# A four-layer graph network on one core: the blocks between layers 1 and 2 as a pipeline of sections in program order, with the normalized input stored and reloaded and the bias added by TensorE

## The chip, the core and the metric

The kernel runs on one core of one Trainium2 chip. TensorE (PE) multiplies matrices and writes to PSUM; VectorE (DVE), ScalarE (ACT) and GpSimd (POOL) work element by element on 128 partitions; SyncE (SP) issues DMAs, as ScalarE and GpSimd can. The engines run side by side, each through its own list of instructions in a fixed order, and wait for one another by semaphores. The metric is the device time of one execution in microseconds (us), as the median of several runs.

## What is computed

12,500 nodes with 128 features and 200,000 edges go through four layers. Each normalizes its input, cuts it at zero, passes messages along the edges and adds the result to its input:

```python
h = jnp.maximum(_layernorm(x, axis=-1), 0.0)
x = x + _L1_gnn_ref(h, edge_attr_3, edge_weight1, L1_gnn_Wq, ..., L1_gnn_Wo, L1_gnn_bo, L1_gnn_ln_g, L1_gnn_ln_b, edge_index)
h = jnp.maximum(_layernorm(x, axis=-1), 0.0)
x = x + _L2_gnn_ref(h, L2_gnn_W, L2_gnn_b, edge_index)
```

The work between the two sums over edges is, from layer 1 (attention with 8 heads),

```python
    attn = attn_exp / (attn_sum[row] + 1e-08)
    out = jax.ops.segment_sum(attn[:, :, None] * v[col], row, num_segments=n)
    out = out.reshape(n, HID) @ Wo.T + bo
    h = x + out
    mu = jnp.mean(h, axis=-1, keepdims=True)
    var = jnp.mean(jnp.square(h - mu), axis=-1, keepdims=True)
    return (h - mu) / jnp.sqrt(var + LN_EPS) * ln_g + ln_b
```

where this `x` is the normalized, cut input `h`; and from layer 2, the degree of each node with itself counted, and rows to be summed over neighbours:

```python
    deg = jax.ops.segment_sum(w, row, num_segments=N) + 1.0
    dinv = jnp.where(deg > 0, jax.lax.rsqrt(deg), 0.0)
```

## The kernel before

The nodes lie in NB = 98 blocks of 128, one node per partition. Most loops run over seven chunks of 14 blocks (`CHUNKS`), and inside them over groups of four, four, four and two (`groups`). A scheduler sets the order of instructions on each engine at compile time, from a model of their costs; inside `tc.manual_schedule()` the program's own order holds. Tiles come from pools: a name with `bufs=n` has n places in a ring, and a place is written again only when all readers of its last content are done.

Before the edges of layer 1, per chunk, the output of layer 0 is finished in `acc` (`layer0_out`), stored to `xd` in DRAM from ScalarE's queue, and normalized (`layernorm_stats`, with `ln` kept). `layer1_table` then makes the table of queries, keys and values: `normed_transposed` (L769) normalizes a block into `h`, a ring of four one-block tiles, TensorE transposes it, and ScalarE copies four transposed blocks out of PSUM. Keys and values go to `kvt`, queries to `qd`, both by DMA from SP. Beside it run the steps of `source_tiles`, which prepare the edge lists with GpSimd's gathers.

The edges of layer 1 (`layer1_edges`) leave per node the weighted sum of values, the sum of weights and the number of edges in `acc` (137 columns per block), and a small `eps`. Two conditional blocks that are not taken end that part. Then `gnn` loads `x` from `xd` by seven DMAs from ScalarE's queue (L2350), and two generators take turns by chunk:

- `layer1_out` (L1805): `rden` is the reciprocal of the sum of weights; `o` (L1822) the weighted mean, by VectorE; `h` is made again from `x` and `ln` (L1826, by the helper's L329 on ScalarE); TensorE transposes `o` (L1827), ScalarE copies it to `ot` (L1830), and TensorE adds `h` times the identity and `ot` times `wo` in PSUM (L1833, L1834). VectorE adds the bias `bo`, spread over all partitions, on the way to `inner` (L1835). GpSimd adds `ln_b` to `x` (L1828). After a whole chunk come its statistics, ScalarE's scaling of `inner` (L1841), GpSimd's product with `ln_g` (L1843) and VectorE's sum into `x` (L1844).
- `layer2_table` (L1894): statistics of `x`, `scaled` by `dinv`, the normalized rows into `acc` (L329 on ScalarE), and `split` (L787): ScalarE casts the rows to f16 and VectorE takes the rest (L792), also as f16. SP stores both in `zt` (L1912).

`layernorm_stats` (L307) takes one BN_STATS per block on VectorE (L313), five small operations (L316 to L320), a square root on ScalarE (L322) and two more on VectorE (L323, L324).

`layer2_edges` waits for all of `zt`. `bucket_places` (L892) loads the places of the edges in buckets (1600 KB, SP) and adds a mask (L899). Then two streams are interleaved: `sum_rows` gathers rows of `zt` by GpSimd (L340) and sums them by TensorE (L1872); `buckets` loads `z` and `lanes` from SP, and makes rows by TensorE (`pout`, L937), ScalarE (`r`, L942) and TensorE again (`sums`, L914). The sums of layer 2's output follow in `layer2_out`; its sum of the bias `b2` into `x` on GpSimd (L1952) needs no sums over edges, and the scheduler puts it beside the work between the layers.

The DVE lines here and in the profile are lines of this kernel; L313 to L329, L340 and L777 are helpers' lines that several stages share.

Of the kernel before, what the change touches and what calls it, by code (L numbers as in the profile page):

```python
# [48 lines left out]
H = 8  # L49
# [47 lines left out]

CHUNK = 14
# [19 lines left out]
class Net:  # L118
# [58 lines left out]
    def later_constants(self, pool, temp, psum):  # L177
# [36 lines left out]
        self.parts = pool.tile([P, 3 * D], BF16, name="biasparts")  # L214
        nc.vector.memset(self.parts, 0.0)
        part = temp.tile([P, 3 * D], BF16, name="biaspart")
        for i in range(3):
            nc.vector.tensor_copy(part, self.bqkv)
            nc.vector.scalar_tensor_tensor(self.parts, part, self.ident[:, i:i + 1], self.parts, op0=OP.mult, op1=OP.add)
            if i < 2:  # L220
                nc.vector.tensor_sub(self.bqkv, self.bqkv, part)
# [9 lines left out]
        self.bo = row("bo", "L1_gnn_bo")  # L231
# [16 lines left out]
        yield  # L248

# [519 lines left out]
    def normed_transposed(self, pool, psum, x, lo, hi, ln):  # L769

        nc = self.nc
        k = hi - lo
        p = psum.tile([P, 4, P], F32, name="pht", bufs=2)
        for j in range(k):
            h = pool.tile([P, D], F32, name="h", bufs=4)
            self.normed(h, x, lo + j, ln)
            nc.tensor.transpose(p[:, j, :], h, self.ident)  # L777
        ht = pool.tile([P, 4, P], F32, name="ht", bufs=2)
        nc.scalar.activation(ht[:, :k], p[:, :k], AF.Copy)
        return ht  # L780
# [687 lines left out]
    def layer1_table(self, work, psum, kv_view, q_view, x, lo, hi, ln):  # L1468
# [4 lines left out]
        ht = self.normed_transposed(work, psum, x, lo, hi, ln)  # L1473
# [331 lines left out]
    def layer1_out(self, x, ln, acc, eps):  # L1805

        nc, tc = self.nc, self.tc
        with tc.tile_pool(name="l1c", bufs=2) as work, tc.tile_pool(name="ps13", bufs=2, space=PSUM) as psum:
            nc.vector.tensor_copy(self.outdeg, acc[:, :, D + H])
            rden = work.tile([P, NB, H], F32, name="rden", bufs=1)  # L1810
            ln2 = self.layernorm(work, "inner")
            for c0, c1 in CHUNKS:
                nc.vector.tensor_add(rden[:, c0:c1, :], acc[:, c0:c1, D:D + H],
                                     eps[:, None, :].to_broadcast([P, c1 - c0, H]))
                nc.vector.reciprocal(rden[:, c0:c1, :], rden[:, c0:c1, :])
                inner = work.tile([P, CHUNK, D], F32, name="inner")
                for lo, hi in groups(c0, c1):
# [564 lines left out]
```

## Time and profile before

| | |
|---|---|
| median of 3 runs | 9729.52 us (9725.72 to 9742.2) |
| profiled execution | 7967.66 us |
| its span, first to last instruction | 7965.0 us |
| mean granted TensorE clock in it | 0.759 |
| busy: PE, DVE, ACT, POOL | 5216.0, 5606.0, 3772.7, 5505.8 us |
| layer 1 table | about 2180 to 2345 us of the span |
| eps of layer 1 done | 4523 |
| last store of zt landed | 4749.8 |
| layer 2 edges | 4750 to about 6910 |

The profile is of one execution. A group of instructions has its line, engine, operation, output and inputs, shapes and number; then its busy time in us and the mean of one in ns; then the idle time of the engine ahead of them, and what ended it. The windows give, for a stretch of time, the busy us and the number of instructions of each engine, the granted TensorE clock, the share of time that the 16 DMA engines were busy, and GB/s. In the timeline a line has its start, its duration, the engine, and in brackets the idle time ahead of it and what it waited for. "PEld" is the loading of weights into TensorE, a "q" after an engine's name its instruction queue.

### The profile page before, as it was taken

What the parts mean: (1) busy time and instruction counts of PE and PEld (TensorE: products, weight loads), DVE (VectorE), ACT (ScalarE), POOL (GpSimd) and SP (SyncE); (2) the same over time, 40 slices, a digit from 0 to 9 for tenths busy, and PEclk for the clock granted to TensorE, in tenths of its full rate; (3) what the DMA queues carried; (4) which work ended last, traced back from release to release, by engine and by line L of the source; (5) the groups of instructions that cost most, each with busy time, mean ns of one, the idle gap of its engine ahead of it and who ended that gap; (6) DMA issues with size and microseconds to landing.
All of it is one profiled execution on the core that took longest, in us unless ns stands there. A gap on an engine that the chain in (4) does not pass through costs nothing. (4 is left out here: it accounts for less than half of the span.)

```text
span 7965.0 us, 123010 instructions
## 1 busy us (share of the span) xinstructions
PE 5216.0 (65%) x36039; PEld 4233.1 (53%) x36040; DVE 5606.0 (70%) x17675; ACT 3772.7 (47%) x8051; POOL 5505.8 (69%) x5641
## 2 busy tenths in 40 slices
PE   4344544444376666666666537776888898768887
PEld 3344444444346666656666536555644554456665
DVE  5687777777667776666666666666766776778887
ACT  4466666666463333223333364443534454456556
POOL 0777777777637777777777557777777766357774
PEclk7566666656586667677676669888988998879999
DMA  6333333333475555555556514443433443445554
GB/s 107 85 83 82 79 83 80 84 79 82 94 222 186 186 185 175 174 175 172 183 179 189 137 61 135 133 127 118 149 115 118 125 132 117 109 120 135 150 150 122
DMA packets 780792, 1038.72 MB, mean 130 GB/s; under 512 B 202181, under 2 KB 548698, under 8 KB 779834
## 3 DMA queue, kind: packets, MB, share of 16 engines
q1 hardware_dynamic: 535039, 543.32, 23.2%
q0 software_dynamic: 202304, 471.89, 22.1%
q10 hardware_dynamic: 42747, 15.32, 0.9%
q8 instruction: 298, 4.88, 0.2%
q14 instruction: 404, 3.31, 0.1%
HBM read 963.63 MB, written 66.40 MB: 129 GB/s over the span
## 5 line engine op out<-in xcount | busy, mean ns | idle before, releaser
L942 ACT ACTIVATE r<-pout 128x512 f16<-128x512 f32 x2352 | 1400.2, 597 | 1268.9 <-PE pout L937 1144.7
L340 POOL DMA_INDIRECT rows<-hw,idxd x1564 | 1492.5, 954 | 674.1 <-issue 449.0
L340 POOL DMA_INDIRECT rows<-zt,idxs x1624 | 1560.0, 961 | 559.2 <-issue 405.0
L340 POOL DMA_INDIRECT rows<-kvt,idxs x1624 | 1591.3, 980 | 494.9 <-issue 418.5
L914 PE MATMUL sums<-yours,r 128*128 128x288 f16 (+1 forms) x9408 | 1875.9, 323 | 3.2 <-DVE yours L939 2.8
L939 DVE TENSOR_SCALAR yours<-iotac,bucketp 128x288 f16<-128x288 f16 (+1 forms) x4704 | 1351.0, 329 | 311.8 <-PE sums L914 286.1
L1372 PE MATMUL psum<-rows,weights 128*128 128x130 f32 x3128 | 731.6, 415 | 638.0 <-ACT weights L1366 526.9
L914 PEld LDWEIGHTS <-r 128*128 128x128 f16 x9408 | 944.5, 101 | 338.5 <-issue 7.0
L1372 PEld LDWEIGHTS psum<-rows,weights 128*128 128x128 f32 x3128 | 658.0, 311 | 676.6 <-ACT weights L1366 587.7
L937 PE MATMUL pout<-z,mine 128*128 128x256 f16 x4704 | 930.3, 281 | 39.2 <-ACT r L942 35.7
L340 POOL DMA_INDIRECT rows<-h,late x620 | 606.8, 979 | 185.4 <-issue 145.5
L1602 ACT ACTIVATE weighted<-lg 128x64 f32<-128x64 f32 x203 | 53.1, 262 | 1438.5 <-DVE lg L1600 1438.5
L1623 PE MATMUL psum<-weighted,hot 128*128 128x137 f32 x3136 | 662.6, 391 | 74.4 <-DVE weighted L1612 73.8
L1596 DVE TENSOR_TENSOR rows<-pq,rows 128x512 f32<-128x512 f32 x406 | 280.5, 691 | 571.0 <-DMA rows<-kvt,idxs 570.4
L1623 PEld LDWEIGHTS psum<-weighted,hot 128*128 128x128 f32 x3136 | 622.4, 290 | 98.6 <-DVE weighted L1612 95.2
L1366 ACT ACTIVATE weights<-off,weight,minus 128x128 f32<-128x128 bf16 x1173 | 483.6, 481 | 336.8 <-DVE minus L1356 202.5
L1583 PE MATMUL pq<-query,mine 128*128 128x128 f16 x3136 | 333.7, 291 | 467.5 <-DVE mine L1552 464.7
L1872 PE MATMUL psum<-rows,hot 128*128 128x128 f16 x3248 | 341.8, 232 | 411.8 <-DMA rows<-zt,idxs 367.4
L937 PEld LDWEIGHTS <-mine 128*128 128x128 f16 x4704 | 450.1, 101 | 272.9 <-issue 54.6
L1583 PEld LDWEIGHTS <-mine 128*128 128x128 f16 x3248 | 306.1, 137 | 498.7 <-DVE mine L1552 495.5
L1870 DVE TENSOR_SCALAR hot<-iotac,places 128x128 f16<-128x128 f16 x1624 | 367.6, 281 | 280.4 <-PE psum L1872 279.1
L1872 PEld LDWEIGHTS <-hot 128*128 128x128 f16 x3248 | 249.8, 103 | 528.9 <-issue 475.0
(497 smaller groups left out, 9240.7 us busy)
## 6 DMA issues: line engine op xcount, KB each, us to landing
near<-lengths SPq DMA_DIRECT2D x203, 512.0 KB
lanes<-lanes SPq DMA_DIRECT2D x112, 896.0 KB
lanes<-slanest SPq DMA_DIRECT2D x203, 256.0 KB
z<-zt SPq DMA_DIRECT2D x112, 448.0 KB
lanes<-lanes SPq DMA_DIRECT2D x196, 256.0 KB
lanes<-dlanes SPq DMA_DIRECT2D x195, 256.0 KB
rows<-kvt,idxs POOLq DMA_INDIRECT x1624
rows<-zt,idxs POOLq DMA_INDIRECT x1624
```

What stands on the lines that cost most here:

```text
L340: self.nc.gpsimd.indirect_dma_start(out=out, out_offset=None, in_=table, in_offset=bass.IndirectOffsetOnAxis(ap=idx[:, t:t + 1], axis=0))
L914: nc.tensor.matmul(sums[i], self.part(r[:, i, :], h), yours[:, i, :], start=s == 0 and h == 0, stop=s == NB - 1 and h == PARTS - 1)
L937: nc.tensor.matmul(p[:, j, :], mine[:, (i + j) * P:(i + j + 1) * P], z[:, s % zb, :], start=True, stop=True)
L939: nc.vector.tensor_scalar(yours[:, j, :], self.iotac[:, :cols], place[:, b:b + 1], None, op0=OP.is_equal)
L942: nc.scalar.activation(r, p, AF.Copy)
L1366: nc.scalar.activation(hot[:, j, :], off, AF.Relu, bias=w[:, j:j + 1], scale=minus[:, j:j + 1])
L1372: nc.tensor.matmul(p, hot[:, j, :], rows[:, j, :n], start=j % G == 0, stop=j % G == G - 1)
L1583: nc.tensor.matmul(pq[:, j, :], s["mine"][i][:, j, :], s["query"][i * G + j][:, h * D:(h + 1) * D], start=h == 0, stop=h == 1)
L1596: nc.vector.tensor_mul(k, s["pq"][i], k)
L1623: nc.tensor.matmul(p, s["hot"][j // G][:, j % G, :], v[:, j, :], start=first and j == 0, stop=last and j == W - 1)
L1870: nc.vector.tensor_scalar(hot, self.iotac[:, :P], place[:, lo + j:lo + j + 1], None, op0=OP.is_equal)
L1872: nc.tensor.matmul(p, hot, self.part(rows[:, j, :], h), start=first and h == 0, stop=last and h == PARTS - 1)
```

## The change

- `layer1_out` and `layer2_table` are replaced by one function, `between`, under `manual_schedule`. It cuts the 98 blocks into 13 sections of eight (`SECTION`; the last has two), and per step t of a loop runs the parts of several sections: the loads of section t + 2, `heads`, `turn`, `add_bias` and `project` of t, `spread` and `scaled_inner` of t - 1, `gain` and `total` of t - 2, `rows` and `rests` of t - 3.
- The normalized input isn't made again: `normed_transposed` has a tile `h` of four blocks in a ring of two, and `layer1_table` stores it to `hd`; `own` loads it as `h2`, a ring of three sections. `x` is loaded by section in the same place, both from SP.
- The bias `bo` is kept as three bf16 parts in three rows (`three_parts`, until now written out for the bias of q, k and v) and enters PSUM by a matmul with ones. There is no copy with bias; `spread` takes its statistics and `scaled_inner` its input from PSUM.
- Of the rests, the first group of each section is GpSimd's, the second VectorE's.
- `bucket_places` for layer 2 runs ahead of `between`, in a pool of its own.

In the diff, the bodies of the two removed functions are left out.

```diff
+SECTION = 8
 CHUNK = 14
...
-        self.parts = pool.tile([P, 3 * D], BF16, name="biasparts")
-        nc.vector.memset(self.parts, 0.0)
...
+        self.parts = self.three_parts(pool, temp, self.bqkv, 3 * D, "bias")
...
-        self.bo = row("bo", "L1_gnn_bo")
+        bo = temp.tile([P, D], F32, name="bo")
+        nc.sync.dma_start(bo, self.rows(a["L1_gnn_bo"], D))
+        self.bo = self.three_parts(pool, temp, bo, D, "bo")
...
+    def three_parts(self, pool, temp, row, n, name):
+        nc = self.nc
+        parts = pool.tile([P, n], BF16, name=f"{name}parts")
+        nc.vector.memset(parts, 0.0)
+        part = temp.tile([P, n], BF16, name=f"{name}part")
+        for i in range(3):
+            nc.vector.tensor_copy(part, row)
+            nc.vector.scalar_tensor_tensor(parts, part, self.ident[:, i:i + 1], parts, op0=OP.mult, op1=OP.add)
+            if i < 2:
+                nc.vector.tensor_sub(row, row, part)
+        return parts
...
-    def normed_transposed(self, pool, psum, x, lo, hi, ln):
+    def normed_transposed(self, pool, psum, x, lo, hi, ln, rows=None):
...
+        h = pool.tile([P, 4, D], F32, name="h", bufs=2)
         for j in range(k):
-            h = pool.tile([P, D], F32, name="h", bufs=4)
-            self.normed(h, x, lo + j, ln)
-            nc.tensor.transpose(p[:, j, :], h, self.ident)
+            self.normed(h[:, j, :], x, lo + j, ln)
+            nc.tensor.transpose(p[:, j, :], h[:, j, :], self.ident)
+        if rows is not None:
+            nc.sync.dma_start(rows[:, lo:hi, :], h[:, :k])
         ht = pool.tile([P, 4, P], F32, name="ht", bufs=2)
         nc.scalar.activation(ht[:, :k], p[:, :k], AF.Copy)
         return ht
...
-    def layer1_table(self, work, psum, kv_view, q_view, x, lo, hi, ln):
+    def layer1_table(self, work, psum, kv_view, q_view, h_view, x, lo, hi, ln):
...
-        ht = self.normed_transposed(work, psum, x, lo, hi, ln)
+        ht = self.normed_transposed(work, psum, x, lo, hi, ln, h_view)
...
-    def layer1_out(self, x, ln, acc, eps):
+    def between(self, dram, pool, x, x_view, h_view, acc, eps):
...
+        zt, z_view = self.table(dram, "zt")
+        dinv = pool.tile([P, NB], F32, name="dinv")
+        sections = [(b, min(b + SECTION, NB)) for b in range(0, NB, SECTION)]
+        wide = [P, SECTION, D]
+        with tc.tile_pool(name="l1c", bufs=2) as work, tc.tile_pool(name="ps13", bufs=2, space=PSUM) as psum, \
+                tc.manual_schedule():
+            rden = work.tile([P, NB, H], F32, name="rden", bufs=1)
+            inner, ln2, scaled = (self.layernorm(work, n) for n in ("inner", "zln", "scaled"))
+            state = [{} for _ in sections]
+
+            def quads(i):
+                return [(b, min(b + 4, sections[i][1])) for b in range(*sections[i], 4)]
+
+            def heads(i):
+                lo, hi = sections[i]
+                r = rden[:, lo:hi, :]
+                nc.vector.tensor_add(r, acc[:, lo:hi, D:D + H], eps[:, None, :].to_broadcast([P, hi - lo, H]))
+                nc.vector.reciprocal(r, r)
+                o = state[i]["o"] = work.tile(wide, F32, name="o")
+                for b, e in quads(i):
+                    nc.vector.tensor_mul(o[:, b - lo:e - lo].rearrange("p g (h d) -> p g h d", h=H),
+                                         acc[:, b:e, :D].rearrange("p g (h d) -> p g h d", h=H),
+                                         rden[:, b:e, :, None].to_broadcast([P, e - b, H, HD]))
+
+            def own(i):
+                lo, hi = sections[i]
+                h = state[i]["h"] = work.tile(wide, F32, name="h2", bufs=3)
+                nc.sync.dma_start(h[:, :hi - lo], h_view[:, lo:hi, :])
+                nc.sync.dma_start(x[:, lo:hi, :], x_view[:, lo:hi, :])
+
+            def turn(i):
+                lo, hi = sections[i]
+                t = state[i]["ot"] = work.tile([P, SECTION, P], F32, name="ot")
+                for b, e in quads(i):
+                    p = psum.tile([P, 4, P], F32, name="pt", bufs=3)
+                    for j in range(b, e):
+                        nc.tensor.transpose(p[:, j - b, :], state[i]["o"][:, j - lo, :], self.ident)
+                    nc.scalar.activation(t[:, b - lo:e - lo, :], p[:, :e - b], AF.Copy)
+
+            def add_bias(i):
+                for b, e in quads(i):
+                    nc.gpsimd.tensor_add(x[:, b:e, :], x[:, b:e, :], self.ln_b[:, None, :].to_broadcast([P, e - b, D]))
+
+            def project(i):
+                lo, hi = sections[i]
+                p = state[i]["po"] = psum.tile(wide, F32, name="po", bufs=2)
+                for j in range(hi - lo):
+                    nc.tensor.matmul(p[:, j, :], self.onesb, self.bo, start=True, stop=False)
+                    nc.tensor.matmul(p[:, j, :], self.ident, state[i]["h"][:, j, :], start=False, stop=False)
+                    nc.tensor.matmul(p[:, j, :], state[i]["ot"][:, j, :], self.wo, start=False, stop=True)
+
+            def spread(i):
+                lo, hi = sections[i]
+                self.layernorm_stats(work, inner, lo, hi, state[i]["po"])
+
+            def scaled_inner(i):
+                lo, hi = sections[i]
+                t = state[i]["in"] = work.tile(wide, F32, name="inner")
+                for b in range(lo, hi):
+                    nc.scalar.activation(t[:, b - lo, :], state[i]["po"][:, b - lo, :], AF.Identity,
+                                         bias=inner[1][:, b:b + 1], scale=inner[0][:, b:b + 1])
+
+            def gain(i):
+                lo, hi = sections[i]
+                for b, e in quads(i):
+                    t = state[i]["in"][:, b - lo:e - lo, :]
+                    nc.gpsimd.tensor_mul(t, t, self.ln_g[:, None, :].to_broadcast([P, e - b, D]))
+
+            def total(i):
+                lo, hi = sections[i]
+                for b, e in quads(i):
+                    nc.vector.tensor_add(x[:, b:e, :], x[:, b:e, :], state[i]["in"][:, b - lo:e - lo, :])
+                self.layernorm_stats(work, ln2, lo, hi, x[:, lo:hi, :])
+                self.scale(scaled, ln2, lo, hi, dinv)
+
+            def rows(i):
+                lo, hi = sections[i]
+                for b in range(lo, hi):
+                    self.normed(acc[:, b, :D], x, b, scaled)
+                z = state[i]["z"] = work.tile([P, SECTION, PARTS, D], PART, name="zparts")
+                nc.scalar.activation(z[:, :hi - lo, 0, :], acc[:, lo:hi, :D], AF.Copy)
+
+            def rests(i):
+                lo, hi = sections[i]
+                z = state[i]["z"]
+                for b, e in quads(i):
+                    at = slice(b - lo, e - lo)
+                    engine = nc.gpsimd if b == lo else nc.vector
+                    engine.tensor_sub(z[:, at, 1, :], acc[:, b:e, :D], z[:, at, 0, :])
+                    nc.sync.dma_start(z_view[:, b:e, :], z[:, at].rearrange("p k h d -> p k (h d)"))
+                state[i].clear()
+
+            def step(f, i):
+                if 0 <= i < len(sections):
+                    f(i)
+
             nc.vector.tensor_copy(self.outdeg, acc[:, :, D + H])
...
+            nc.vector.tensor_add(dinv, self.indeg, self.outdeg)
+            nc.vector.tensor_scalar_add(dinv, dinv, 1.0)
+            nc.scalar.activation(dinv, dinv, AF.Sqrt)
+            nc.vector.reciprocal(dinv, dinv)
+            for t in range(-2, len(sections) + 3):
+                step(own, t + 2)
+                step(gain, t - 2)
+                step(heads, t)
+                step(rows, t - 3)
+                step(turn, t)
+                step(add_bias, t)
+                step(project, t)
+                step(spread, t - 1)
+                step(scaled_inner, t - 1)
+                step(total, t - 2)
+                step(rests, t - 3)
+        return zt, dinv
 
...
-    def layer2_table(self, dram, pool, x, acc, chunks):
...
-            place = self.bucket_places(work, places, over)
+            place = self.place
...
+        self.place_open.close()
...
+    hd_view = dram.tile([NP, D], F32, name="hd").rearrange("(b p) d -> p b d", p=P)
...
     x = xpool.tile([P, NB, D], F32, name="x")
-    for lo, hi in CHUNKS:
-        nc.scalar.dma_start(x[:, lo:hi, :], xd_view[:, lo:hi, :])
-    zt, dinv = net.layer2_table(dram, late, x, acc, net.layer1_out(x, ln, acc, eps))
+    net.place_open = ExitStack()
+    net.place = net.bucket_places(net.place_open.enter_context(tc.tile_pool(name="bplace", bufs=1)), places, over)
+    zt, dinv = net.between(dram, late, x, xd_view, hd_view, acc, eps)
     y = net.layer2_edges(dram, zt, acc, edges, dbins, (*slists[:2], oblocks), pairs, lanes, places, over)
```

## The prediction

> **What bounds the kernel now.** I read the page first, then a table of windows over the stage between the layers, its instruction groups by form, its chain in order of time, and last the same views of the two neighbours that the change reaches: the layer-1 table stage and the start of layer 2.
>
> ```profile
> span 7965.0 us, 123010 instructions
> core 0: us, PE busy (x) PEld busy (x) DVE busy (x) ACT busy (x) POOL busy (x), PEclk, DMA share, GB/s
> 2220.00:2240.00 20.00, 13.01 (x48) 7.13 (x47) 13.66 (x66) 11.89 (x40) 15.87 (x16) 0.92 0.99 305
> ...
> 4520.00:4540.00 20.00, 1.97 (x8) 1.57 (x8) 10.27 (x27) 0.00 (x0) 0.55 (x1) 0.50 0.89 220
> ...
> 4620.00:4640.00 20.00, 6.72 (x32) 6.20 (x32) 18.01 (x49) 13.80 (x35) 13.07 (x10) 0.65 0.09 26
> 4640.00:4660.00 20.00, 7.20 (x36) 6.96 (x36) 15.16 (x42) 14.71 (x38) 10.74 (x9) 0.59 0.11 33
> ...
> L329 ACT ACTIVATE h<-x,ln,ln 128x128 f32<-128x128 f32 x98 | 41.5, 481 | 4.9 <-PE po L1833 4.1 <-ACT ot L1830 0.7
> L1843 POOL TENSOR_TENSOR inner<-inner,ln_g 128x512 f32<-128x512 f32 x21 | 28.7, 1379 | 27.3 <-ACT inner L1841 12.2 <-issue 8.4 <-DVE o L1822 6.7
> L1844 DVE TENSOR_TENSOR x<-x,inner 128x512 f32<-128x512 f32 x21 | 26.4, 1256 | 15.4 <-POOL inner L1843 15.4
> L1835 DVE TENSOR_TENSOR inner<-po,bo 128x512 f32<-128x512 f32 x21 | 14.3, 682 | 25.8 <-PE po L1834 25.8
> ```
>
> The windows say where the limit lies. In 4520 to 4540 ScalarE does nothing: it is issuing seven loads of x. From 4543 on no engine is full; VectorE comes nearest, at 15 to 18 of 20 us. The last four lines are groups of the stage 4518 to 4752. The sum L1844 (512 columns) has a mean of 1256 ns, while the sum of the same size out of PSUM (L1835) takes 682: the first was held up. In order of time the pattern is plain:
>
> ```profile
> 4523.37 18.59 ACTq L2350 DMA_DIRECT2D x<-xd  x7
> 4541.99 1.28 ACT L329 ACT_TABLE_LOAD   x1 [26.02 <-DMA x<-xd]
> ...
> 4620.65 0.69 DVE L1844 TENSOR_TENSOR x<-x,inner 128x512 f32<-128x512 f32 x1 [1.10 <-POOL inner L1843]
> 4622.49 1.74 DVE L1844 TENSOR_TENSOR x<-x,inner 128x512 f32<-128x512 f32 x1 [0.18 <-POOL inner L1843]
> ...
> 4766.80 1.88 DVE L899 TENSOR_SCALAR bucketp<-bucketp,bnone 128x3200 f32<-128x3200 f32 x1
> ...
> 4772.52 1.06 PE L937 MATMUL pout<-z,mine 128*128 128x256 f16 x4
> ```
>
> The same sum takes 0.69 us with GpSimd idle and 1.74 beside it. The chain repeats every 56.2 us for two chunks (POOL inner at 4563.15, 4619.36, 4675.46), so 28.2 us per 14 blocks, 16.1 per 8. The last store lands at 4749.8, the first gather follows at 4750.8. So the stage lasts 226 us: a head of 20, some 196 in the rhythm, and a tail of 10.8 from the last `scaled` (4739.0).
>
> **What the Trainium skill says.** SBUF — State Buffer, Who interferes with whom: a VectorE instruction with two SBUF inputs and a GpSimd instruction that reads SBUF exclude each other; the second waits for the whole first. The 0.69 against 1.74 us agrees. VectorE: DVE Perf Modes, The TRN2 errata: ScalarE pays less fixed time per instruction from PSUM than from SBUF. The trace agrees: 0.29 us for 128 columns from PSUM (L1478), 0.48 from SBUF (L329). DMA: Bandwidth & Descriptors, Issuing engines are not separate DMA queues: loads from ScalarE and SyncE share the same engines. Moving x to SP thus frees ScalarE, not the bus.
>
> **The change part by part.**
>
> Head. Removed: seven issues on ScalarE (18.6 us). On SP there now stand bucketp (1600 KB), then h2 and x of each section (512 KB each). At the rate of before (6272 KB in 18.6 us, 345 KB/us) bucketp and h2(0) need 6.3 us, with some 2 us to land: 4532. Meanwhile VectorE does o of sections 0 and 1 and L899 (1.9 us), done by about 4534. TensorE projects section 0 at the low clock in about 1 us per block (two matmuls at 0.43, the trace's pitch at 4546, and about 0.1 for the bias): 4540. The first statistics of before started at 4549.6.
>
> ScalarE. Removed: 98 h (41.5 us). The 98 inner go from SBUF to PSUM source, about 0.3 instead of 0.39 us. Per 8 blocks: rows 8 x 0.40, inner 8 x 0.30, two ot at 0.5, one cast of 1024 columns at about 1.05, two roots at 0.3: 8.3 us. Not the bound.
>
> TensorE. Added: 98 bf16 bias matmuls and their weight loads, estimated at 0.1 to 0.2 us each from L1476 (0.34 us for 384 columns) and 0.108 for its load: 10 to 20 us in all. Per 8 blocks 8 x (0.25 transposed + 0.86 + 0.15) = 10 us at the low clock. Below the step; nothing.
>
> GpSimd. Per 8 blocks: two gains, two ln_b, two b2 (the compiled order leaves those inside the stage, as before) and one new rest: 7 x 1.27 = 8.9 us (before: 13.6 per 14, 7.8 per 8). The new one queues before the next gain, and gain before `total`; it waits for ScalarE's cast, early in a step.
>
> VectorE. Removed: the bias add (17.2 us with its short form) and half of the rests (about 12). Added: 13 sections instead of 7 chunks, so six more sets of small operations, twice: before 24.7 us for 7, so about 21 us more. Unhindered, per 8 blocks: heads 1.9, spread 2.45 (8 statistics at 0.20, five small at 0.1, root result 0.35), total 3.9, rest 0.6, two round trips to ScalarE at 0.4: 9.7 us.
>
> The step. Operations that need the shared port: GpSimd 8.9 plus VectorE's two-input ones (o 1.2, x sum 1.2, rest 0.6, small 1.6) 4.6: 13.5 us, which I take as the floor of a step. By the same count before has 13.6 + 8.05 = 21.7 of its 28.2 us, so 12.4 of 16.1 per 8 blocks: 3.7 us lay outside the lock, in waits along the chain. With three sections under way most of these have a step of slack; the root round trips and small operations behind GpSimd remain. I take 2 us over the floor, 15.5; the ends are 13.5 and 17.2 (3.7 kept).
>
> Sum of the stage: spread(0) ends 4541; step 2 without rests 12 us, 4553; nine steps of 15.5, 4692.5; step 12 with a quarter section 13.5, 4706; step 13 7.5, 4713.5; tail (rows and cast of section 11 on ScalarE 4.3, then those of 12, its rest behind a b2 on GpSimd, and a store) 10.5: 4724. Against 4749.8: 26 us gained. At 13.5 a step 45, at 17.2 10.
>
> Start of layer 2. bucketp no longer stands before z and lanes: before, L899 came at 4766.8 and the first pout at 4772.5, 22 us after the stores. Without those 1600 KB, at the 190 KB/us of 4750 to 4800, it could come some 8 us earlier, with L899 gone from VectorE's order 10. But GpSimd's gathers run without a gap from 4750.8 (1.25 us each) and set the pace here, so in the profile it is worth 0; if TensorE sets the pace, up to 10. I take 4.
>
> Table of layer 1. Added: 28 stores of h (6272 KB), and h is a ring of two quads that its store must leave, instead of four blocks. The stage lasts 165 us, 5.9 per quad, with DMA at 0.5 to 0.8 for most of it, but 0.99 in 2220 to 2240, where one wait of ScalarE for a qd store lasted 14.9 us. A store of 256 KB issued on SP among kv and q stores has about a quad to land. Least 0; most some 25 (1.3 MB more in the full stretch at 305 KB/us is 4 us, and one more wait like the 14.9). I take 3. The layer-0 table has the new ring without the store: 0. The rest of the orders is alike on all engines.
>
> Total: 26 + 4 - 3 = 27 us. Against its own time, 7967.66 becomes about 7941. The median of the runs, 9729.52, lies 1762 us above the profiled execution, which these views don't explain; a lower TensorE clock than the profile's 0.759 would do (5216 us busy become 7918 at 0.5). The steps above are VectorE's, GpSimd's and ScalarE's, so I carry the 27 us over as they are: 9703. A measurement of this kernel can't tell less than 0.2% (19.5 us) from no change.
>
> **The rivals.**
> No change: a step stays at 17.2 us, because small operations with two inputs each lose a turn to GpSimd (for it: 1.24 us for a 14-column L316 at 4635.28; against: most of them took 0.17). 10 + 2 - 4 = 8 us gained: 9721.
> A larger gain: the lock is kept full (13.7 a step, 43 us) and layer 2 is paced by TensorE, so that the bucketp load counts whole (10): 53 us, 9677. For it: TensorE is at 0.9 busy from 6000 to 6600; against: the gathers' pace before 5700.
> Slower: the two-quad ring in the table stage. If SP's order holds an h store behind kv or q stores that wait for VectorE (such waits of SP, 31.6 us in 11, are in its list), ScalarE stalls per quad. At 2 us for each of 28 quads it costs 56, net 29 slower: 9759. It decides from 1.1 us per quad on. Against it: most stores there are issued within 0.4 us.
> That the pipeline doesn't do what it says is answered by the compiled order: program order holds on all engines.
>
> **How the numbers follow.** Forecast 0.50, no change 0.20, larger gain 0.17, slower 0.13. The forecast's own range, 9687 to 9716, lies mostly beyond 0.2%: 0.41 of its 0.50. Faster: that 0.41 and the larger gain's 0.17, 0.58. Slower: its 0.13 and 0.02 of the second case, 0.15. Same: the rest, 0.27. The range reaches to the larger gain and into the slower case: 9668 to 9742.
>
> **What would show it.** First statistics of the stage near 4540; nine even steps near 15.5 us between `total`s; no ScalarE issue of x; the last zt store some 26 us earlier after the eps; first pout 12 to 14 us after it instead of 22; the table stage at 165 to 170 us. Steps of 17 and VectorE's small operations at over 1 us would make it wrong, and so would ScalarE waiting for hd stores.

## The result, and the profile after

| | before | after |
|---|---|---|
| median of 12 runs each | 9730.92 us | 9726.76 us |
| lowest to highest | 9719.07 to 9755.38 | 9712.42 to 9742.62 |
| ratio of the runs, 95% interval | | 0.9993, 0.9984 to 1.0002 |
| profiled execution, its span | 7967.66, 7965.0 us | 9735.01, 9733.2 us |

No measurable change: 4 us between the medians, where 27 were forecast. The two spans can't be set against each other. The profile of before shows an execution of 7968 us (a short one, from here on), that of after one of 9735 (a long one), of the length of the timed runs. So I compare stage by stage first, and then with traces of before of both lengths, which the experiments brought.

In the changed kernel, these are windows of the stage between the layers, to set beside those of 4620 to 4660 of before:

```profile
core 0: us, PE busy (x) PEld busy (x) DVE busy (x) ACT busy (x) POOL busy (x), PEclk, DMA share, GB/s
5569.00:5589.00 20.00, 10.95 (x69) 9.89 (x67) 18.52 (x56) 11.46 (x30) 12.75 (x11) 0.72 0.44 119
5589.00:5609.00 20.00, 11.47 (x71) 10.35 (x70) 18.50 (x57) 11.32 (x29) 13.62 (x11) 0.76 0.29 79
5609.00:5629.00 20.00, 12.21 (x63) 10.86 (x64) 18.91 (x53) 13.45 (x31) 13.92 (x11) 0.67 0.55 141
```

VectorE (the third engine) is busy 18.5 to 18.9 of 20 us, where it had 15 to 18. Five of its and GpSimd's groups in that stage, by form, show which waits went and what the busy time is made of:

```profile
L1886 POOL TENSOR_TENSOR inner<-inner,ln_g 128x512 f32<-128x512 f32 x24 | 30.7, 1279 | 36.4 <-ACT inner L1879 35.7
L1840 DVE TENSOR_TENSOR o<-acc,rden 128x512 f32<-128x512 f32 x24 | 24.9, 1079 | 0.4
L322 DVE BATCH_NORM_STATS2 st<-po 128x6 f32<-128x128 f32 x98 | 20.6, 278 | 5.3 <-PE po L1869 5.3
L328 DVE TENSOR_TENSOR std<-std 128x8 f32<-128x8 f32 x24 | 15.6, 650 | 0.0
L1891 DVE TENSOR_TENSOR x<-x,inner 128x512 f32<-128x512 f32 x24 | 15.5, 685 | 0.0
```

The sum into x, L1891, waits for nothing (15.4 us before, for GpSimd) and takes 685 ns instead of 1256. L328, an operation on eight columns, takes 650 ns on average: most of that is not work but a wait inside it (it takes 0.16 us where GpSimd is idle, as a timeline of f1_after shows below). Ends of the stage, from the rows of `eps`, `z` and `pout` (shortest, median and longest duration in ns, first and last start):

```profile
L2410 DVE COPY eps<-eps x1: 171/171/171, 5548.8 to 5548.8; 128x8 f32<-128x8 f32 x1
L936 SPq DMA_DIRECT2D z<-zt x112: 360/371/434, 5739.2 to 8433.5; - x112
L948 PE MATMUL pout<-z,mine x4704: 269/273/421, 5751.9 to 9661.9; 128*128 128x256 f16 x196
```

I measure the stage from the copy of `eps` to the first load of `z`: 190.4 us here, 227.2 in the profile of before. The first `pout` follows 12.7 us after the load, instead of 22.1. The stores of `hd` run from 2648.1 to 2794.5, and ScalarE waited for them 6.2 us in all. The stage gained more than was forecast and layer 2 started as forecast, and yet the median hardly moved.

### The profile page after: what moved, and what is told of

Read it like the earlier page. It is cut to its first block, busy times and chain, and to the rows that moved or that the text cites. A ratio compares the mean times of both kernels' runs of the same rounds, so it can differ in the third digit from the quotient of the medians.

```text
span 9733.2 us, 123233 instructions
## 1 busy us (share of the span) xinstructions
PE 5617.8 (58%) x36137; PEld 4459.3 (46%) x36138; DVE 5596.7 (58%) x17742; ACT 3701.7 (38%) x7946; POOL 5484.9 (56%) x5648
## 5 line engine op out<-in xcount | busy, mean ns | idle before, releaser
L953 ACT ACTIVATE r<-pout 128x512 f16<-128x512 f32 x2352 | 1367.7, 597 | 2075.4 <-PE sums L925 730.4
L925 PE MATMUL sums<-yours,r 128*128 128x288 f16 (+1 forms) x9408 | 1962.2, 334 | 12.6 <-issue 6.4
L948 PE MATMUL pout<-z,mine 128*128 128x256 f16 x4704 | 960.8, 289 | 812.7 <-issue 436.2
L948 PEld LDWEIGHTS <-mine 128*128 128x128 f16 x4704 | 459.9, 102 | 1149.0 <-issue 931.6
L1634 PE MATMUL psum<-weighted,hot 128*128 128x137 f32 x3136 | 726.5, 383 | 340.2 <-issue 315.1
L1587 PE MATMUL pb<-we,near 128*128 128x16 f32 x3248 | 583.0, 307 | 565.7 <-issue 553.7
L1587 PEld LDWEIGHTS pb<-we,near 128*128 128x128 f32 x3248 | 601.9, 267 | 598.9 <-issue 581.9
L1386 DVE SCALAR_TENSOR_TENSOR acc<-psum,mask,acc 128x130 f32 x782 | 270.3, 346 | 523.3 <-remote 345.0
L1602 DVE TENSOR_TENSOR add<-pb,lengthst 128x64 f32<-128x64 f32 x203 | 45.1, 222 | 785.5 <-remote 592.6
L942 DVE TENSOR_SCALAR mine<-lanes,lane 128x512 f16<-128x512 f16 x1176 | 431.8, 368 | 83.7 <-PE sums L925 40.8
```

Of the source, the lines that this page charges most:

```text
L925: nc.tensor.matmul(sums[i], self.part(r[:, i, :], h), yours[:, i, :], start=s == 0 and h == 0, stop=s == NB - 1 and h == PARTS - 1)
L942: nc.vector.tensor_scalar(mine[:, :n * P], lane[:, s % zb, :n * P], self.lane, None, op0=OP.is_equal)
L948: nc.tensor.matmul(p[:, j, :], mine[:, (i + j) * P:(i + j + 1) * P], z[:, s % zb, :], start=True, stop=True)
L953: nc.scalar.activation(r, p, AF.Copy)
L1386: nc.vector.scalar_tensor_tensor(d[:, h, :], p, mask[:, 2 * s + i, h:h + 1], d[:, h, :], op0=OP.mult, op1=OP.add)
L1587: nc.tensor.matmul(pb[:, j].rearrange("p a h -> p (a h)"), s["near"][:, j * P:(j + 1) * P], self.we.rearrange("p a h -> p (a h)"), start=F ...
```

## The experiments

Twelve runs follow, in five groups, each on another chip with the kernel before beside it. On four chips all runs of before took 7941 to 7984 us, on the fifth its two runs took 9588 and 9615, so the length seems to go with the chip. The runs of the result are of the long kind. Differences are to the median of before on the same chip. The stage is measured as above; the table of layer 1 runs from the first sum into `acc` of `layer0_out` (L1463 of before) to the last issue of a store of `kvt`.

| run | us | to before (95%) | stage | first pout after it | table of layer 1 |
|---|---|---|---|---|---|
| before, e0_before | 7963.85 | | 227.2 | 22.2 | 158.9 |
| before, h1_before | 9587.83 | | 227.2 | 22.1 | 157.4 |
| changed, f1_after | 7935.73 | -40.1 (-50 to -29) | 191.2 | 13.2 | 159.1 |
| changed, h2_after | 7912.18 | -35.1 (-45 to -24) | 191.1 | 13.3 | 158.3 |
| e1_delay | 7982.07 | +16.6 (+9 to +23) | 238.8 | 12.3 | 158.9 |
| e2_remake | 7942.02 | -23.5 (-35 to -15) | 203.2 | 12.8 | 158.7 |
| e3_early | 7964.08 | -1.4 (-8 to +6) | 226.3 | 13.2 | 160.3 |
| f2_bias | 7949.95 | -25.9 (-38 to -18) | 199.0 | 12.5 | 158.0 |
| f3_serial | 8115.25 | +139.4 (+124 to +149) | 364.7 | 13.3 | 160.0 |
| g1_ten | 7925.93 | -42.8 (-55 to -28) | 181.6 | 12.2 | 158.9 |
| g2_rests | 7940.53 | -28.2 (-38 to -18) | 195.8 | 12.5 | 158.6 |
| g3_b2late | 7941.68 | -27.0 (-37 to -18) | 181.8 | 12.7 | 158.6 |

The time of the stage repeats within 1 us from chip to chip (227.2 in all three traces of before; 191.2, 191.1 and, in the long execution, 190.4 in the changed kernel), while whole runs of one kernel on one short chip spread by up to 20 us. So small differences are read from the stages.

**e0_before**: before, unchanged.

> The kernel before, unchanged, for a second trace. The profile shown of it had a span of 7965 us while all its timed runs lie near 9730; the changed kernel's profile spans 9733. Theory A (the stage between the layers gained about 36 us in these longer executions too, and what follows gives it back): span near 9730, the stage from eps to the last store of zt 215 to 235 us against 190 after, and the gathers and edges of layer 2 some 30 us shorter than in the changed kernel. Theory B (the longer execution has another balance, and the stage gained little there): span near 9730, stage below 205 us, all else alike. Theory C (the table of layer 1 lost what the stage gained): stage 215 to 235, and the table stage of layer 1 some 25 us or more shorter than in the changed kernel.

It came out at 7963.85 us, of the short kind, so it answers nothing about the long one. It shows that the stage of 227 us repeats.

**e1_delay**: is a time in the stage passed on to the end?

```diff
+DELAY = 75
...
+            for _ in range(DELAY):
+                nc.vector.tensor_copy(rden, acc[:, :, D:D + H])
             for t in range(-2, len(sections) + 3):
```

> The changed kernel with 75 needless copies of 784 columns on VectorE ahead of the first section, 30 to 65 us in which all of the stage waits. Theory A (what follows the stage is limited by something that doesn't begin with the stage's end): the time changes by less than a third of the delay, under 20 us. Theory B and theory C (the stage's end sets all that follows): the whole delay shows in the time, 30 to 65 us.

The stage is 47.6 us longer than the changed kernel's (238.8 to 191.2), and the time 56.7 us further from before than f1_after's and 51.7 than h2_after's. Within the intervals of both that is the whole delay. Theory A, that what follows does not begin with the end of the stage, falls for executions of this kind.

**e2_remake**: h again from x by ScalarE; no store, and the old ring of four one-block tiles in the table of layer 1 (that part of the edit is not shown).

```diff
-                nc.sync.dma_start(h[:, :hi - lo], h_view[:, lo:hi, :])
                 nc.sync.dma_start(x[:, lo:hi, :], x_view[:, lo:hi, :])
+            def again(i):
+                lo, hi = sections[i]
+                h = state[i]["h"] = work.tile(wide, F32, name="h2", bufs=3)
+                for b in range(lo, hi):
+                    self.normed(h[:, b - lo, :], x, b, ln)
...
+                step(again, t + 1)
```

> The changed kernel without the store and reload of the normalized input: the table of layer 1 has the old ring of four one-block tiles and no store, and ScalarE makes h2 again from x in the pipeline, one section ahead. Adds 3.8 us of ScalarE per section of 15 in the stage. Theory C: the table of layer 1 becomes 25 us or more shorter and the time falls by 20 to 35 us. Theories A and B: the time stays within 10 us, the table stage within 8.

The table of layer 1 takes 158.7 us without the stores and 159.1 with them: the stores and the new ring cost nothing here, and theory C falls for executions of this kind. The stage is 12 us longer: 7 of them in its head (its first `total` came 32.6 us after the copy of `eps`, 25.6 in f1_after), 5 in nine steps of 14.7 instead of 14.2 us. Storing h is worth about 12 us.

**e3_early**: the kernel before with `bucket_places` ahead of the stage.

```diff
-            place = self.bucket_places(work, places, over)
+            place = self.place
...
+        self.place_open.close()
...
+    net.place_open = ExitStack()
+    net.place = net.bucket_places(net.place_open.enter_context(tc.tile_pool(name="bplace", bufs=1)), places, over)
     for lo, hi in CHUNKS:
         nc.scalar.dma_start(x[:, lo:hi, :], xd_view[:, lo:hi, :])
```

> The kernel before with one part of the change: the places of the edges in buckets loaded and masked ahead of the stage between the layers. Theory A: no measurable change, within 10 us, although the first pout comes 8 to 10 us earlier after the last store of zt. Theories B and C: some 4 to 10 us faster.

The first `pout` comes 9 us earlier, layer 2's edges (first load of `z` to the last `pout` of the class rows) take 2144.4 us instead of 2149.9, and the time can't be told from before. With 4 to 6 us at stake, the interval leaves both readings open.

**f1_after**: the changed kernel beside before.

> The changed kernel, unchanged, on the chip where the kernel before takes 7965 us. The delayed one took 7982, and its trace has 51 us of copies (4526.8 to 4578.4) ahead of the stage. If a time at the stage goes through to the end in executions of this length (theory D: the gain is real and whole here, and lost only in executions of 9730 us, which idle in every stage), 7925 to 7940. Theory A (given back after the stage in any execution): 7955 to 7970. Its table of layer 1 should last 159 us as in all four runs so far, and its stage 186 to 190.

40.1 us faster, as theory D has it; the stage gives 36.0 of it. So the forecast of 27 is rather low on these chips, and the puzzle is only the long executions.

**f2_bias**: VectorE adds the bias from PSUM to SBUF.

```diff
-                    nc.tensor.matmul(p[:, j, :], self.onesb, self.bo, start=True, stop=False)
...
+                    nc.vector.tensor_add(t[:, b - lo:e - lo, :], state[i]["po"][:, b - lo:e - lo, :],
+                                         self.bo[:, None, :].to_broadcast([P, e - b, D]))
```

> The changed kernel with the bias added by VectorE on the way from PSUM to SBUF, as before, and no bias matmuls: statistics and the scaling of inner then read SBUF. VectorE gets two sums of 0.68 us per step, 1.4 us, and ScalarE 0.1 us more per block. If VectorE's own work sets the step of 13 us (18.5 of 20 us busy), the stage grows by 13 x 1.4 = 18 us, the time by 15 to 22. If the lock with GpSimd sets it, as the forecast took it, a sum from PSUM falls beside GpSimd's work and the time changes by less than 8.

The stage grows by 7.8 us, 0.84 per full step where VectorE got 1.36, and the time by 14.2 against f1_after: between the two theories. Part of the new sums seems to fit where VectorE would have waited; which waits became shorter isn't shown.

**f3_serial**: the sections one after another.

```diff
-                step(gain, t - 2)
                 step(heads, t)
-                step(rows, t - 3)
...
-                step(spread, t - 1)
-                step(scaled_inner, t - 1)
-                step(total, t - 2)
-                step(rests, t - 3)
+                step(spread, t)
+                step(scaled_inner, t)
+                step(gain, t)
+                step(total, t)
+                step(rows, t)
+                step(rests, t)
```

> The changed kernel with all parts of one section after one another in program order, and no sections side by side: the same instructions, another order. If the overlap is what brings the gain, each section costs its own chain, about 22 to 28 us, and the stage lasts 290 to 360 us, 100 to 170 more than with overlap. If the gain comes from the work removed (h, the bias, the issues of x), the stage stays below 230 us.

A section costs 28.3 to 29.6 us, the stage 364.7, just above what was expected of the overlap. Program order alone makes the stage far worse than the scheduler's order did (227); the same instructions with four sections side by side take 191. In one section of it, VectorE's timeline shows the waits that the overlap fills:

```profile
4643.77 0.69 DVE L1891 TENSOR_TENSOR x<-x,inner 128x512 f32<-128x512 f32 x1 [3.04 <-POOL inner L1886]
4645.61 0.69 DVE L1891 TENSOR_TENSOR x<-x,inner 128x512 f32<-128x512 f32 x1 [1.15 <-POOL inner L1886]
...
4653.88 0.71 DVE L1908 TENSOR_TENSOR zparts<-acc,zparts 128x512 f16<-128x512 f32 x1 [4.40 <-ACT zparts L1900]
...
4667.19 1.68 DVE L322 BATCH_NORM_STATS2 st<-po 128x6 f32<-128x128 f32 x8 [8.18 <-PE po L1869]
```

In VectorE's timeline of f1_after, on the same chip, the sum into x has no bracket, since what it reads is a step old; only the root's round trip to ScalarE is left:

```profile
4651.98 0.16 DVE L328 TENSOR_TENSOR std<-std 128x8 f32<-128x8 f32 x1
4652.17 0.17 DVE L329 SCALAR_TENSOR_TENSOR stv<-std,stv 128x8 f32<-128x8 f32 x1
4652.71 0.20 DVE L332 RECIPROCAL inner<-inner 128x8 f32<-128x8 f32 x1 [0.37 <-ACT inner L331]
4652.94 0.17 DVE L333 SCALAR_TENSOR_TENSOR inner<-sts,inner 128x8 f32<-128x8 f32 x1
4653.03 1.29 DVE L1891 TENSOR_TENSOR x<-x,inner 128x512 f32<-128x512 f32 x2
```

**g1_ten**: sections of ten.

```diff
-SECTION = 8
+SECTION = 10
...
-                h = state[i]["h"] = work.tile(wide, F32, name="h2", bufs=3)
+                h = state[i]["h"] = work.tile(wide, F32, name="h2", bufs=2)
...
-                    p = psum.tile([P, 4, P], F32, name="pt", bufs=3)
+                    p = psum.tile([P, 4, P], F32, name="pt", bufs=2)
```

> The changed kernel with sections of ten blocks (ten sections instead of thirteen), with two places instead of three for h2 and pt, so that it fits. If the small operations, paid once per section, cost what the trace shows in VectorE's order (about 4 us per section with what they wait behind GpSimd), three sections fewer take 8 to 14 us off the stage of 191, less about 5 for a longer head and tail: 3 to 9 us faster than the changed kernel. If the shared port sets the step whatever the sections' size, within 4 us.

The stage falls by 9.6 us to 181.6, as expected if the small operations are paid once per section. It is the fastest of the kernels against before, though the 42.8 us can't be told from the changed kernel's 40.1 and 35.1 by the times alone.

**g2_rests**: all rests on VectorE.

```diff
-                    engine = nc.gpsimd if b == lo else nc.vector
-                    engine.tensor_sub(z[:, at, 1, :], acc[:, b:e, :D], z[:, at, 0, :])
+                    nc.vector.tensor_sub(z[:, at, 1, :], acc[:, b:e, :D], z[:, at, 0, :])
```

> The changed kernel with all rests on VectorE again (0.69 us each there, 1.12 on GpSimd). If the port that VectorE and GpSimd share sets the step, as the forecast took it, the step falls by 1.12 - 0.69 = 0.4 us and the stage by about 5 of 191. If VectorE's own list sets it, each step grows by 0.69 and the stage by about 8.

The step, as the mean of nine between the `total`s, goes from 14.16 to 14.84 us: by 0.68, the price of one rest on VectorE. The 1.12 us that GpSimd no longer needs buy nothing. The first and the tenth `total` of f1_after, then those of g2_rests:

```profile
4554.20 1.29 DVE L1891 TENSOR_TENSOR x<-x,inner 128x512 f32<-128x512 f32 x2
4681.60 1.29 DVE L1891 TENSOR_TENSOR x<-x,inner 128x512 f32<-128x512 f32 x2
```

```profile
4546.93 1.29 DVE L1891 TENSOR_TENSOR x<-x,inner 128x512 f32<-128x512 f32 x2
4680.47 1.29 DVE L1891 TENSOR_TENSOR x<-x,inner 128x512 f32<-128x512 f32 x2
```

The stage grows by only 4.6, as its head and tail get shorter.

**g3_b2late**: the sum of `b2` after the sum over edges.

```diff
-                    nc.gpsimd.tensor_add(x[:, lo:hi, :], x[:, lo:hi, :], self.b2[:, None, :].to_broadcast([P, k, D]))
                     nc.vector.tensor_add(m, m, acc[:, lo:hi, :D])
...
                                                        x[:, lo + j, :], op0=OP.mult, op1=OP.add)
+                    nc.gpsimd.tensor_add(x[:, lo:hi, :], x[:, lo:hi, :], self.b2[:, None, :].to_broadcast([P, k, D]))
```

> The changed kernel with the sum of layer 2's bias b2 into x put after the sum of layer 2's output, so that its 28 operations of GpSimd (36 us) can't run in the stage between the layers. If the shared port sets the step of 13 us, two sums of 1.27 us fewer per step make it about 10.5 and the stage 25 to 30 us shorter; the layer-2 output stage, VectorE 18 to 19 of 20 us busy there, gets longer by 5 to 15. In all 10 to 25 us faster than the changed kernel. If GpSimd's operations only fill VectorE's gaps, the stage stays within 5 us of 191, and the time does not fall.

Two of GpSimd's sums fewer, 2.5 us of the shared port, shorten the step by 0.77, to 13.39, and the stage by 9.4. The layer-2 output stage (from the last `pout` of the class rows to the next `bucketp`) grows by some 14 us, to 156.5 from the 141.8 and 142.3 of g1_ten and g2_rests on the same chip (139 to 145 in all others), and takes all of it back.

**h1_before**: before again, for the long kind.

> The kernel before, unchanged, once more, in the hope of an execution near 9730 us like those that the result was taken from: on the three chips of the experiments so far it took 7960 to 7985. If it is one of 9730: its stage between the layers at 226 to 228 us, as in the other two traces of it, would say that the stage's gain of 36 us was there too in the executions of the result, and that the edges around it gave it back; a stage near 190 would say that there was no gain to give. If it is one of 7960: stage 227, table of layer 1 159, layer 2's edges 2150, within 1, 1 and 5 us.

This one came to the long chip, where a second run of before took 9615.33 us. Its rows of `eps` and `z`:

```profile
L2341 DVE COPY eps<-eps x1: 172/172/172, 5411.4 to 5411.4; 128x8 f32<-128x8 f32 x1
L925 SPq DMA_DIRECT2D z<-zt x112: 370/371/2117, 5638.6 to 8311.8; - x112
```

227.2 us again. The stage of before is as long in a long execution as in a short one, and so the changed kernel's 190.4 is a gain of 36.8 us in the result's kind too. What makes an execution long is in the loops of gathers. From the pages of e0_before, then h1_before, then the changed kernel of the result:

```profile
L340 POOL DMA_INDIRECT rows<-hw,idxd x1564 | 1493.7, 955 | 673.5 <-issue 448.0
L340 POOL DMA_INDIRECT rows<-zt,idxs x1624 | 1560.0, 961 | 558.8 <-issue 403.0
L340 POOL DMA_INDIRECT rows<-kvt,idxs x1624 | 1586.2, 977 | 495.0 <-issue 407.0
...
L937 PE MATMUL pout<-z,mine 128*128 128x256 f16 x4704 | 928.5, 281 | 39.6 <-ACT r L942 36.0
L1623 PE MATMUL psum<-weighted,hot 128*128 128x137 f32 x3136 | 678.7, 398 | 84.5 <-DVE weighted L1612 84.2
```

```profile
L340 POOL DMA_INDIRECT rows<-zt,idxs x1624 | 1571.1, 967 | 1115.3 <-issue 414.1
...
L340 POOL DMA_INDIRECT rows<-kvt,idxs x1624 | 1590.2, 979 | 941.4 <-DVE weighted L1612 478.2
L340 POOL DMA_INDIRECT rows<-hw,idxd x1564 | 1491.8, 954 | 1079.9 <-issue 422.6
...
L937 PE MATMUL pout<-z,mine 128*128 128x256 f16 x4704 | 956.3, 287 | 770.7 <-issue 355.6
...
L1576 PE MATMUL pb<-we,near 128*128 128x16 f32 x3248 | 568.5, 302 | 496.4 <-issue 487.5
...
L1623 PE MATMUL psum<-weighted,hot 128*128 128x137 f32 x3136 | 691.5, 379 | 219.5 <-issue 193.0
```

```profile
L349 POOL DMA_INDIRECT rows<-zt,idxs x1624 | 1559.0, 960 | 1147.3 <-issue 412.1
L349 POOL DMA_INDIRECT rows<-kvt,idxs x1624 | 1588.4, 978 | 1033.5 <-DVE weighted L1623 568.0
...
L349 POOL DMA_INDIRECT rows<-hw,idxd x1564 | 1487.1, 951 | 1131.6 <-issue 423.6
...
L948 PE MATMUL pout<-z,mine 128*128 128x256 f16 x4704 | 960.8, 289 | 812.7 <-issue 436.2
```

The gathers take the same time, the idle time between them grows by 1.6 to 2 times. The 0.3 us of "issue" ahead of each gather are not what grows (403 and 414 us for `zt`); a small number of longer waits, most of them put down to other engines, is. TensorE stands out: all its idle time put down to "issue", where it waited for nothing that the trace names, is 82 us in e0_before and 1761 us in h1_before, much of it ahead of short matmuls (L1576). Gathers of layer 1 that land late are not the reason: VectorE's L1596, which reads their rows, waited 560.2 us for them in e0_before and not at all in h1_before. Why TensorE starts late isn't shown.

By the starts of the first and last gather, the loops of layers 0 to 3 take 1972, 2144, 2114 and 819 us in e0_before and 2374, 2593, 2682 and 964 in h1_before: 1562 of the 1624 us between the two spans. The table of layer 1, the stage between the layers and the layer-2 output stage are the same in both, within 3 us.

**h2_after**: the changed kernel again, for the long kind.

> The changed kernel, unchanged, once more, in the hope of a chip on which the kernel before takes 9600 to 9730 us. If it is one: theory E (the stage's gain of 36.8 us is there, 227.2 in the kernel before against 190.4, and the loops of gathers vary by chip, and cover it in the result): 27 to 45 us faster than the kernel before on the same chip. Theory F (the gather loop of layer 1 is slower in the changed kernel in such executions, since hd shifts the tables in DRAM; in the two slow traces it takes 3.5% longer than in the kernel before, the others 0.8 to 2.0%): under 15 us faster, and the loop of layer 1 again some 30 us longer than the other loops would have it. If it is a chip of 7960: 30 to 45 us faster, as before.

It came to a short chip: 35.1 us faster, a repeat of f1_after. Theories E and F stay undecided.

## Why the prediction was right or wrong

**Head.** Forecast: first statistics near 4540, 17 us after `eps` (4523.4 there). Measured 14.7 us after its copy in f1_after and 13.8 in the profile after. Right, with 2 to 3 us to spare; the mask on `bucketp` ran in that gap, hidden.

**The step.** Forecast 15.5 us, floor 13.5 by the shared port. The nine full steps between `total`s of f1_after take 14.16 us (4554.20 to 4681.60). The size was 1.3 us off; the reason was wrong in part. By the port's account, g2_rests should have made the step 0.4 us shorter and g3_b2late 2.5; they gave 0.68 longer and 0.77 shorter. The sum of all operations that need the port did not set the step (the forecast's 13.5 us become 11.0 without the two sums of g3_b2late, and the step there took 13.39): what bounds it is VectorE's own list, lengthened by the waits for the port that fall inside it. The page SBUF — State Buffer, Who interferes with whom, of the Trainium skill holds as far as these traces show: single operations are blocked (L328 at 650 ns on average, 0.16 us where GpSimd is idle at 4651.98). Comparing the means of o, L325, L328, L329 and `zln` in f1_after with their unblocked times (0.69, 0.17, 0.16, 0.17, 0.17), about 41 of the 191 us are such waits, an estimate.

**ScalarE and TensorE.** Neither sets the step, but two prices were off. The forecast read 0.29 against 0.48 us as the gain of a source in PSUM; but L1478 is a plain copy and L329 has a scale and a bias per partition. The same operation from SBUF (f2_bias), then from PSUM (f1_after):

```profile
L1880 ACT ACTIVATE inner<-inner,inner,inner 128x128 f32<-128x128 f32 x98 | 39.1, 481 | 7.7 <-DVE inner L331 7.7
```

```profile
L1879 ACT ACTIVATE inner<-po,inner,inner 128x128 f32<-128x128 f32 x98 | 35.6, 468 | 7.7 <-DVE inner L333 7.7
```

That is 13 ns less per operation, or 0.04 us of busy time: `inner` took 0.36 us of busy time each where 0.30 was forecast. The bias matmuls, estimated at 10 to 20 us in all, took 25.3.

**The stage's sum.** From `eps` to the end of the first `total` (its `scaled`, 4561.2) it took 32.4 us where 29.6 were forecast; the nine steps 127.4 instead of 139.5; the two short steps and the tail 31.2 instead of 31.5. So the stage gains 36.0 us where 26 were forecast, nearly all of the difference from the term of the step.

**Start of layer 2.** Forecast: first `pout` 12 to 14 us after the last store instead of 22, worth 4. Measured 12.2 to 13.3 after the load of `z`: right. The 4 us aren't shown. Layer 2's edges take 2.9 us less than in e0_before in f1_after and 5.5 in e3_early, but 2.7 more in f3_serial, which has the same early places; over the ten kernels that have them they range from 2144.4 to 2152.6 us.

**Table of layer 1.** Forecast a loss of 3 us, up to 25. Measured 159.1 against 158.9: none, so the rival of the two-quad ring is out on the short chips. In the long executions it is 165.1 in the changed kernel against 157.4 in h1_before, in two executions that may not share a chip; up to 8 us may be lost there.

**Carrying the gain to the median: the step that failed.** The forecast put 27 us into 7967.66 and carried them "over as they are" to 9729.52, with a lower TensorE clock as the guess for the 1762 us between the two. On the chips where the kernel takes 7947 to 7976 us the sum holds, and is even low: 40 and 35 us. In the result's executions 4 us arrived, by the ratio's interval 16 less to 2 more than before. The guess on the clock was wrong: from e0_before to h1_before it fell only from 0.753 to 0.723, and TensorE's busy time rose from 5223.2 to 5572.0 us, by 349 us where the execution is 1624 us longer. The rest is idle time in the loops of gathers, of which the forecast had no trace.

Where some 30 us went in the result stays open. Three things narrow it, all from the changed kernel's long trace and h1_before's. The stage did gain 36.8 us there. It wasn't given back right after the stage: with the first gather at 0, gather 400 of layer 2 starts at 626.3 us in the changed kernel's long trace and at 627.3 in h1_before's. And the loop of layer 1 is 90 us longer than in h1_before, 3.5%, where the loops of layers 0, 2 and 3 are 2.0, 0.8 and 1.9% longer. That may be a cost of the change, since `hd` lies ahead of the tables in DRAM; but the two traces may come from different chips, the loop of layer 0, with not one changed instruction, differs by 47 us between them, and on the short chips layer 1 shows nothing (2172 to 2186 us from the table's last store to `eps` in the changed kernels, 2176 to 2180 in before). TensorE's idle time without a named reason, between the first and the last gather of that loop, is 995 us in the changed kernel and 887 in h1_before, so the 90 us may come with the long execution and not with the change.

Nor is it known on which chips the result's runs were. The medians of before on two short chips differ by 29 us (7947.24 and 7975.83), and the long runs of before by over 100 us (9588 to 9615 in h1_before's group, 9719 to 9755 in the result). If the result's runs of before and after were not on one chip, the missing 30 us may be a difference of chips. Both kernels on one long chip would decide it; there is no such pair.

That the time lay inside the range of 9668 to 9742 is luck: it lies outside the 9687 to 9716 of the forecast's own account, and the range was wide only to take in the larger gain and part of the slower case. "Same", which came out, had been given 0.27, "faster" 0.58. The time is close to the number of the "no change" case, 9721, but that case's mechanism, steps staying at 17.2 us, did not happen; nor did that of the slower case. The stage came out nearer the "larger gain".

## What to carry to other kernels

When the profiled execution and the timed runs differ by a fifth, a sum made in the profile is a forecast for that execution only: first find which stages hold the difference, and ask whether what is being sped up feeds one of them. A pipeline written in program order wins by the overlap, not by the order (191 against 365 us with the same instructions), and once one engine is busy 18.5 of 20 us, price an edit first by what it adds to or takes off that engine's own list (0.68 us of the 0.69 added in g2_rests, 0.84 of 1.36 in f2_bias), and only then by a sum over a shared port, which gave 0.77 of 2.5 us in g3_b2late. An operation moved out of a full stage must be priced where it lands too, as the bias of layer 2 showed.

## What the runs showed of the hardware that was not expected

- The same kernel takes 7941 to 7984 us on four chips and 9588 to 9615 on a fifth. Between one trace of each kind, the busy times of VectorE, ScalarE and GpSimd agree within 1% (TensorE's is 7% longer, at a clock of 0.723 instead of 0.753), and so do the stages without gathers, within 2%; the four loops of gathers take 18 to 27% longer, with the same 0.95 to 0.98 us per gather and up to twice the idle time between them. What causes the idle time isn't shown: TensorE's own idle time for no reason that the trace names grows from 82 to 1761 us.
- A bias matmul of 128 columns in bf16 among float32 matmuls took 259 ns, 25.3 us for 98, on a TensorE that was busy 11 to 12 of 20 us; the same bias on VectorE cost the stage 7.8 us.
- Small operations grow most in proportion beside GpSimd: one of 8 columns takes 0.16 us alone and up to 1.23 us behind one of GpSimd's (L328 at 4641.75 of f1_after).
